# Six node tiles or four in the first phase of a two-layer graph network, the other two as a short group among the later ones

## The chip, the core and the metric

The kernel runs on one core of one Trainium2 chip. The metric is the device time of one execution in microseconds. Everything below comes from one program on one core, timed three times, and from one further execution that was recorded by the hardware profiler.

## What is computed

There are 4096 nodes with 512 features each and a sparse 4096 x 4096 adjacency matrix of float32 weights. Two layers follow each other, and each adds its result to x:

```python
h = jnp.maximum(_layernorm(x, axis=-1), 0.0)
x = x + _L0_gnn_ref(h, adj, L0_gnn_W, L0_gnn_b)
h = jnp.maximum(_layernorm(x, axis=-1), 0.0)
x = x + _L1_gnn_ref(h, adj, L1_gnn_W, L1_gnn_a, L1_gnn_wtrans)
```

The first layer is a dense product with the normalised adjacency:

```python
rowsum = adj.sum(axis=1)
d_inv_sqrt = jnp.where(rowsum > 0, rowsum ** (-0.5), 0.0)
normalized_adj = d_inv_sqrt[:, None] * adj * d_inv_sqrt[None, :]
return jax.nn.relu(normalized_adj @ x @ W + b)
```

The second layer is graph attention over the nonzero entries of the adjacency: `softmax(where(adj > 0, leaky_relu(Wh1 + Wh2.T), -1e12))` and its negative counterpart, each multiplied with the node features, joined and multiplied with `wtrans`, and an elu.

## The kernel before

**Tiles.** The 4096 nodes are 32 node tiles of 128 nodes. Layer 0 computes, for each destination tile i, the sum over the 32 source tiles j of adj_t[j, i] times y0[j], where y0[j] is d[j] times (normalised x[j]) W. W is multiplied first (`project`), d is applied when the product leaves the accumulator (`scale`, line 708).

**The list that the change edits.** `GROUPS` (line 24) says in which order and in what portions the destination tiles are worked: (first tile, number of tiles). Before, it is one group of six (tiles 26 to 31), six groups of four and one of two.

**First phase (lines 927 to 990), the first entry of GROUPS.** It runs once over the 32 source tiles j. For each j it reads the row tile of the adjacency (four loads of 512 KB, `ar`, on SP's queue) to sum the degrees, reads x[j] (GpSimd's queue), normalises and transposes it on TensorE (`turn_x`), multiplies with W (`project`, 4 matmuls of 128x512), and multiplies the first group's adjacency columns with y0[j] (`multiply`, line 858, one matmul of 128x512 for each node tile in the group). The columns come as one load `at` for each j, as wide as the group, from a pool of five buffers. Each accumulator of the first group holds one of the eight PSUM banks through the whole phase; `turn_x` and `project` use the banks that are left.

**Later groups (`group`, line 1038).** All y0 are there by now, and the product is done in 2x2 blocks by a seven-product scheme: two source tiles and two destination tiles at a time, seven products of 128x128x256 for what would be four of 128x128x512. The loop goes over 16 pairs of source tiles, jp. With four destination tiles, one jp is 14 products; with two it is 7. VectorE makes the sums of adjacency blocks that the scheme needs (`sum_at`, four operations for each load), and in the first such group the sums of y0 too (`sum_y`). A load `at` is 512 KB in either case: two source tiles by four destination tiles, or four by two (`nj = 8 // n`). The pool has six such buffers.

**What a group does for the one before it.** At the start of a group, VectorE joins the accumulators of the group before (`join_blocks`, or `evict` for the first phase) into one y per node tile. In the following steps jp = 0, 1, ... `finish0` turns each y into the node's new row: it adds x, writes `x1_dram`, takes the layer norm (line 642, ScalarE), makes two dot products (line 822, VectorE) and writes the row into eight copies of a table, one write on GpSimd's queue and seven on ScalarE's (`put_row`, line 443). The row is held in a tile `h` with two buffers, so the third row of a group can be made only when the first one's eight writes have landed. At jp = 8 `spread_s` (line 837) transposes the dot products of the finished tiles on TensorE; this matmul needs the dots of all of them.

**Masks.** `pack` turns each adjacency load into bytes (ScalarE, line 722; VectorE in the first phase, line 724) and writes them to the tables. `EARLY` (line 26) names three groups whose masks are made ahead of their turn, in the group with the given index, from loads of their own.

**Order.** A scheduler orders the instructions of each engine within what the program allows; [...] a DMA issue on ScalarE's or SP's list stands in that list like any other instruction.

**After layer 0.** Neighbour lists made in the groups with index 3 and 5 (`make_lists`) feed gathers from the tables, and `sparse_layer1` does the attention for 31 pairs of row blocks.

Of the kernel before, what the change touches and what calls it, by code (L numbers as in the profile page):

```python
# [8 lines left out]
F32 = mybir.dt.float32  # L9
# [10 lines left out]
P = 128  # L20
IB = 512


GROUPS = ((26, 6), (16, 4), (20, 4), (0, 4), (4, 4), (8, 4), (12, 4), (24, 2))

EARLY = {(24, 2): (2,), (12, 4): (3,), (8, 4): (4,)}
PAIR0 = 16
Y_PARTS = (8, 11, 13)
T_PARTS = (7, 9)
# [230 lines left out]
def gcn_gat_kernel(  # L260
# [24 lines left out]
    N, F = x.shape  # L285
# [15 lines left out]
    TT = RPT * RB // P  # L301
    late0, n_late = GROUPS[-1]
    tab0 = PAIR0 // TT
# [8 lines left out]
    def bank(name):  # L312
        return ps.tile([P, 512], F32, tag="ps", name=name)
# [4 lines left out]
    with sbuf(name="init", bufs=1) as init:  # L318
        column = init.tile([P, P], F32, name="column")
        nc.vector.memset(column[:, 0:1], 0.0)  # L320
        n = 1
# [120 lines left out]
    def put_row(queue, g, j, h):  # L442
        return queue.dma_start(  # L443
            out=rows_of(g, j // EJ)[:, j % EJ, :ROW_W], in_=h.bitcast(I32)
        )
# [77 lines left out]
    with sbuf(name="y0", bufs=1) as y_pool, sbuf(name="wa", bufs=1) as wa_pool, sbuf(name="bits", bufs=4) as bits_pool, sbuf(name="small0", bufs=4) as small, ExitStack() as rest, ExitStack() as lists:  # L523
# [16 lines left out]
        keys, lst = {}, {}  # L540
# [206 lines left out]
        def mark():  # L747
            while marking:
                tc.keep_in_program_order(marking.pop(0)())
# [5 lines left out]
        def affine(y, acc, j):  # L755

            nc.vector.scalar_tensor_tensor(y, acc, d_all[:, j : j + 1], b_bc, ALU.mult, ALU.add)
            return y

        def new_y(work, j, k):  # L760
            if k < 0:
                return work.tile([P, F], F32, tag="y", name=f"y{j}", bufs=4)
            if k == 0:
                spare.append(make_pool.tile([P, 3, F], F32, tag="keys", name="spare"))
            return spare[0][:, k]

        def evict(i0, acc, work, _):

            return {
                i0 + k: affine(new_y(work, i0 + k, k - 3), a, i0 + k) for k, a in enumerate(acc)  # L770
            }

        def join_blocks(i0, n, acc, work, new_w):

            ys = {}
            for x in range(n // 2):
                p16, p23, p45, p7 = acc[x]
                j0, j1 = i0 + x, i0 + n // 2 + x
                ys[j0], ys[j1] = y, v = [new_y(work, j, -1) for j in (j0, j1)]
                w = new_w(f"w{j0}")[:, :H]  # L780
                nc.vector.tensor_copy(y[:, :H], p16[:, :H])
                nc.vector.tensor_tensor(w, p16[:, H:], y[:, :H], ALU.add)  # L782
                nc.vector.tensor_tensor(y[:, H:], p45[:, H:], w, ALU.add)

                def first(p23=p23, y=y):
                    nc.vector.tensor_tensor(y, p23, y, ALU.add)

                def second(p7=p7, w=w, p45=p45, v=v):
                    two = "p (a f) -> p a f"
                    nc.vector.tensor_tensor(w, p7, w, ALU.add)  # L790
                    nc.vector.tensor_tensor(
                        v.rearrange(two, a=2),
                        p45.rearrange(two, a=2),
                        w.unsqueeze(1).to_broadcast([P, 2, H]),
                        ALU.add,
                    )

                if n == 2:
                    first()
                    affine(y, y, j0)  # L800
                    second()
                    affine(v, v, j1)
                else:
                    second()
                    first()
            if n > 2:
                for j, y in ys.items():
                    affine(y, y, j)
            return ys

        def finish0(work, j, y, h, prod):
# [15 lines left out]
            put_row(nc.gpsimd, tab0, j, h)  # L827
            if all(not j0 <= j < j0 + n for j0, n in GROUPS[-2:]):
                for g in others:
# [96 lines left out]

        i0, n = GROUPS[0]
        with sbuf(name="w0", bufs=1) as w0_pool, sbuf(name="ain", bufs=9) as ain, sbuf(name="xs", bufs=5) as x_pool, sbuf(name="at6", bufs=5) as at_pool, sbuf(name="bits6", bufs=3) as bits6, sbuf(name="ln", bufs=3) as ln_pool:
# [39 lines left out]
            acc = [bank(f"acc{i0 + k}") for k in range(n)]  # L968
            for j in range(NJ):
# [18 lines left out]
                pack(bits6, i0, j, ats.pop(j), j < 2)  # L988
                mark()
        pending = (GROUPS[0], partial(evict, i0, acc))  # L990
        listing, joining, spare = [], [], []

        def make_lists(g):
            make_keys(g)

            def rows_and_joins(c):
                count_listed(g, c, lst[g])
                li = table_rows(g, c, lst[g])
                joining.extend(partial(join, g, li, m) for m in range(c * NE, (c + 1) * NE))
                if c == 2:  # L1000
                    joining.append(partial(deal, g))

            for n, (c, r) in enumerate(steps):
                listing.append(partial(list_round, keys[g], lst[g], n))
                if n == 5:
                    listing.append(partial(make_places, g))
                if r + 1 == CAPS[c] // 8:
                    listing.append(partial(rows_and_joins, c))

        def judge():  # L1010
# [25 lines left out]
            return verdict  # L1036

        def group(b, work, at_pool, sum_pool, step, prod, n_h=2):

            nonlocal pending  # L1040
            i0, n = GROUPS[b]
            nj = 8 // n
            (p0, pn), take = pending
            order = [p0 + k for k in ((0, 2, 1, 3) if b > 1 else range(pn))]
            ats, sums = {}, {}

            def prepare(jp):
                if 2 * jp % nj == 0:
                    ats[jp] = load_at(at_pool, i0, n, 2 * jp, nj)
                    sums[jp] = sum_at(sum_pool, ats[jp], n, f"sums{i0}_{jp}")  # L1050
                else:
                    ats[jp], sums[jp] = ats[jp - 1], sums[jp - 1]
                if b == 1:
                    sum_y(jp)

            prepare(0)
            for j in order[:2]:
                if j not in xrs:
                    load_xr(j)
            for jp in range(NP):  # L1060
                if jp + 1 < NP:
                    prepare(jp + 1)
                mark()
                if jp == 0:
                    ys = take(work, prod)
                    p7 = bank(f"p7_{i0}")
                    acc = [
                        [*(bank(f"p{k}_{i0 + x}") for k in (16, 23, 45)), p7[:, x * H : (x + 1) * H]]
                        for x in range(n // 2)
                    ]  # L1070
                multiply_blocks(acc, n, jp, ats[jp], sums[jp])
                if (i0, n) not in EARLY:
                    pack(bits_pool, i0, 2 * jp, ats[jp])
                for (e0, m), when in EARLY.items():
                    if b in when:
                        pack(bits_pool, e0, 2 * jp, load_at(at_pool, e0, m, 2 * jp, 2))
                if jp < pn:
                    j = order[jp]
                    h = work.tile([P, ROW_W], F32, tag="h", name=f"h{j}", bufs=n_h)
                    finish0(work, j, ys.pop(j), h, prod)  # L1080
                    if jp + 2 < pn:
                        load_xr(order[jp + 2])
                if jp == 8:
                    spread_s(p0, pn)
                if jp == NP - 4:
                    for k in (0, n // 2):
                        load_xr(i0 + k)
                step(jp)
            pending = (GROUPS[b], partial(join_blocks, i0, n, acc))

# [5 lines left out]
        make_pool = lists.enter_context(sbuf(name="make", bufs=1))  # L1096
        with sbuf(name="work0", bufs=2) as work, sbuf(name="sums", bufs=3) as sum_pool, sbuf(name="at", bufs=6) as at_pool:

            def prod(name):
                return work.tile([P, F], F32, tag="q", name=name, bufs=1)  # L1100

            for b in range(1, len(GROUPS) - 1):

                def step(jp):
                    if jp == 2 and b in (3, 5):
                        make_lists((1, 0)[b == 5])
                    for _ in range((2, 3)[b == 6] if jp != 2 else 0):
                        if listing:
                            listing.pop(0)()
                    if joining:  # L1110
                        joining.pop(0)()

                group(b, work, at_pool, sum_pool, step, prod)
            while listing:
                listing.pop(0)()
            while joining:
                joining.pop(0)()
# [7 lines left out]
        with sbuf(name="work2", bufs=2) as work, sbuf(name="sums2", bufs=2) as sum_pool, sbuf(name="at2", bufs=4) as at_pool, sbuf(name="scratch", bufs=1) as scratch, sbuf(name="pair", bufs=1) as pair:  # L1125
# [100 lines left out]
            k = late0 % EJ  # L1226
# [204 lines left out]
```

## Time and profile before

| what | value |
|---|---|
| time before, median of 3 runs | 2124.37 us (2120.07 to 2126.74) |
| the profiled execution's own time | 2135.61 us |
| its span, first to last instruction | 2133.8 us |
| TensorE busy over the span | 2010.4 us (94%) |
| VectorE, ScalarE, GpSimd busy | 53%, 24%, 43% |
| first phase, to the last line-858 matmul | 336 us |
| groups of four and the group of two | 336 to about 1037 us |
| attention layer at its steady pace | 1330 to 2134 us |

The stage borders are read from where the matmuls of line 858 end and where those of line 899 begin and end. Time outside the span is 1.8 us. The page's busy time of TensorE counts modelled ends of pipelined matmuls; the distance from one matmul's start to the next is the safer measure of its cost. In this profile one float32 matmul shows as two records.

### The profile page before, as it was taken

Reading aid. Unit: us, or ns where it says so; the run is one execution under the profiler, and the core shown is the slowest. Engines: PE = TensorE matmul, PEld = TensorE weight load, DVE = VectorE, ACT = ScalarE, POOL = GpSimd, SP = SyncE. Lnnn points to the kernel's source line nnn. Section 1 sums busy time; section 2 is a strip of 40 time slices with the busy share of each in tenths; the row PEclk is TensorE's granted clock in tenths of the full one; section 3 lists DMA queues with packets and bytes.
Section 4 is the critical chain, followed back from the end, with each engine's and each line's share of the span. In section 5 each row is a group of like instructions: output and inputs, shape, how many; then the busy total and the mean of one; then the engine's idle time right before and its main releaser. Section 6 shows DMA issues by size and latency. Waiting matters only on the chain.

```text
span 2133.8 us, 20055 instructions
## 1 busy us (share of the span) xinstructions
PE 2010.4 (94%) x6456; PEld 1184.6 (56%) x6456; DVE 1121.2 (53%) x2805; ACT 511.8 (24%) x876; POOL 923.9 (43%) x988
## 2 busy tenths in 40 slices
PE   6999999999898989899878998999999999999998
PEld 3444447888787768787434443444444444444443
DVE  5444526463896469835644435445445445445441
ACT  4645612223232310001111212122122122122120
POOL 2010001111123310322467667777777777677740
PEclk9999999999999999999989999999999999999999
DMA  9988918786977875556587778888888888887850
GB/s 372 372 309 320 365 47 281 266 305 199 344 241 251 260 258 172 169 167 199 164 284 238 241 227 265 262 281 243 276 254 272 248 276 246 239 247 235 239 168 21
DMA packets 188041, 524.12 MB, mean 246 GB/s; under 512 B 25235, under 2 KB 34419, under 8 KB 187926
## 3 DMA queue, kind: packets, MB, share of 16 engines
q0 software_dynamic: 71296, 275.22, 41.7%
q1 hardware_dynamic: 88480, 196.46, 27.1%
q10 hardware_dynamic: 28150, 51.07, 6.7%
q8 instruction: 52, 0.85, 0.2%
q14 instruction: 63, 0.52, 0.1%
HBM read 430.83 MB, written 102.92 MB: 250 GB/s over the span
## 4 chain that ended last, share of the span: by engine, by line
PE 47%; DVE 6%; DMA 4%; POOL 4%; issue 3%; ACT 1%; ACTq 1%; another core or an unknown queue 0%; DVEq 0%; SPq 0%; POOLq 0%
PE u L1306 30%; PE o L1329 10%; PE p L899 5%; POOL g L457 4%; DMA at<-in_adj_t 2%; DMA g<-table,idx 1%; DVE keys L393 1%; PE tp L514 1%; DVE lst L391 1%; DMA table<-h 1%; ACTq L443 1%; PE u L1182 1%; ACT m L722 1%; DVE p L488 0%
## 5 line engine op out<-in xcount | busy, mean ns | idle before, releaser
L457 POOL DMA_INDIRECT g<-table,idx x704 | 753.4, 1070 | 266.6 <-issue 197.6
L1306 PE MATMUL u<-g,p 128*128 128x512 f32 x1736 | 766.7, 598 | 14.9 <-DVE p L488 9.7
L1306 PEld LDWEIGHTS u<-g,p 128*128 128x128 f32 x1736 | 326.8, 191 | 405.5 <-issue 382.2
L469 DVE TENSOR_TENSOR z<-g,s 128x512 f32<-128x512 f32 (+1 forms) x124 | 77.4, 624 | 422.6 <-DMA g<-table,idx 376.0
L899 PE MATMUL p<-t,sums 128*128 128x256 f32 x832 | 249.7, 385 | 15.9 <-DVE sums L887 12.8
L899 PE MATMUL p<-y,sums 128*128 128x256 f32 x832 | 253.6, 387 | 6.3 <-DVE sums L889 5.5
L899 PE MATMUL p<-y,at 128*128 128x256 f32 x832 | 253.9, 387 | 3.9 <-DMA at<-in_adj_t 2.6
L1329 PE MATMUL o<-wt_sb,ut 128*128 128x512 f32 x512 | 230.5, 603 | 0.9 <-ACT ut L518 0.5
L479 ACT ACTIVATE p<-z 128x896 f32<-128x896 f32 (+2 forms) x136 | 116.1, 903 | 313.3 <-DVE z L475 156.7
L899 PEld LDWEIGHTS p<-t,sums 128*128 128x128 f32 x832 | 160.1, 193 | 39.5 <-DVE sums L887 14.0
L899 PEld LDWEIGHTS p<-y,sums 128*128 128x128 f32 x832 | 161.5, 194 | 31.1 <-DVE sums L889 6.3
L899 PEld LDWEIGHTS p<-y,at 128*128 128x128 f32 x832 | 160.1, 194 | 30.9 <-issue 3.4
L858 PE MATMUL acc<-y,at 128*128 128x512 f32 x384 | 174.9, 593 | 2.4 <-ACT y L708 2.4
L488 DVE SCALAR_TENSOR_TENSOR p<-g,p 128x384 f32<-128x384 uint8 (+1 forms) x256 | 143.6, 620 | 60.8 <-ACT p L479 30.4
L733 POOL DMA_DIRECT2D table<-m x71 | 54.3, 766 | 251.9 <-ACT m L722 146.6
L1329 PEld LDWEIGHTS o<-wt_sb,ut 128*128 128x128 f32 x512 | 96.7, 194 | 111.9 <-issue 111.0
L722 ACT ACTIVATE m<-at 128x1024 uint8<-128x1024 f32 (+1 forms) x110 | 105.0, 987 | 181.2 <-DMA at<-in_adj_t 140.2
L899 PE MATMUL p<-t,at 128*128 128x256 f32 x416 | 127.0, 388 | 18.8 <-DVE w L782 17.7
L685 PE MATMUL yp<-w_sb,hx_t 128*128 128x512 f32 x256 | 122.2, 623 | 18.1 <-ACT y L708 15.8
L1315 ACT ACTIVATE us<-u,rl 128x512 f32<-128x512 f32 x62 | 42.5, 686 | 389.4 <-issue 237.8
L858 PEld LDWEIGHTS acc<-y,at 128*128 128x128 f32 x384 | 70.5, 190 | 80.5 <-issue 76.9
L886 DVE TENSOR_TENSOR sums<-at 128x256 f32<-128x256 f32 x104 | 43.3, 416 | 136.4 <-PE p L899 67.3
(183 smaller groups left out, 1720.3 us busy)
## 6 DMA issues: line engine op xcount, KB each, us to landing
at<-in_adj_t SPq DMA_DIRECT2D x136, 512.0 KB
ar<-in_adj SPq DMA_DIRECT2D x128, 512.0 KB
table<-h ACTq DMA_DIRECT2D x182, 258.0 KB
table<-m POOLq DMA_DIRECT2D x55, 256.0 KB
at<-in_adj_t SPq DMA_DIRECT2D x32, 384.0 KB
g<-table,idx POOLq DMA_INDIRECT x704
xr<-in_x SPq DMA_DIRECT2D x32, 256.0 KB
x<-x1d SPq DMA_DIRECT2D x32, 256.0 KB
```

The costliest lines, as they stand in the source:

```text
L457: nc.gpsimd.indirect_dma_start(out=gt[:, k, :], out_offset=None, in_=table[2 * n // RPT], in_offset=bass.IndirectOffsetOnAxis(ap=idx[n // ...
L469: return nc.vector.tensor_tensor(z, t.to_broadcast([P, n, RB]), s.unsqueeze(1).to_broadcast([P, n, RB]), ALU.add)
L479: i = nc.scalar.activation(p[:, :, g, :], z, AF.Exp, scale=(1.0, -1.0)[g])
L488: nc.vector.scalar_tensor_tensor(e, m, 0.0, e, ALU.is_gt, ALU.mult)
L685: nc.tensor.matmul(yp, hx_t[j][:, c * P : (c + 1) * P], w0_sb[:, c, :], start=c == 0, stop=c == FC - 1,)
L722: nc.scalar.activation(m, at, AF.Sign)
L733: nc.gpsimd.dma_start(out=rows_of(t, e)[:, c:, ROW_W + (a - t * TT) * P // 4 : ROW_W + (b - t * TT) * P // 4], in_=masks[i0][:, c:, (a - i ...
L858: nc.tensor.matmul(a, at[:, 0, it * P : (it + 1) * P], y0[j], start=j == 0, stop=j == NJ - 1)
L886: op(t[:, 0], a[:, :, 0, 1], a[:, :, 1, 1], ALU.add)
L899: i = nc.tensor.matmul(out, left[:, x * P : (x + 1) * P], right, start=jp == 0 and first, stop=jp == NP - 1 and (final or not first),)
L1306: nc.tensor.matmul(u, p[:, k0 + k].rearrange("p g c -> p (g c)"), gt[:, k, :F].bitcast(F32), start=k0 + k == 0, stop=k0 + k == nk - 1,)
L1329: nc.tensor.matmul(po, ut[:, g, c, :], wt_sb[:, g * FC + c, :], start=g == 0 and c == 0, stop=g == 1 and c == FC - 1,)
```

## The change

The first phase takes tiles 28 to 31 only. Tiles 26 and 27 become a group of two, third in the list, between (16, 4) and (20, 4). The groups after it keep their order, and the indices in `EARLY` and in the code that makes the lists move by one, so that this work stays with the same groups. `pack` is called once for each load, which matters only for a group of two that isn't in `EARLY`. The four y of the first phase fit in the four ordinary buffers, so the spare tile goes.

```diff
-GROUPS = ((26, 6), (16, 4), (20, 4), (0, 4), (4, 4), (8, 4), (12, 4), (24, 2))
-
-EARLY = {(24, 2): (2,), (12, 4): (3,), (8, 4): (4,)}
+GROUPS = ((28, 4), (16, 4), (26, 2), (20, 4), (0, 4), (4, 4), (8, 4), (12, 4), (24, 2))
+
+EARLY = {(24, 2): (3,), (12, 4): (4,), (8, 4): (5,)}
...
-        def new_y(work, j, k):
-            if k < 0:
-                return work.tile([P, F], F32, tag="y", name=f"y{j}", bufs=4)
-            if k == 0:
-                spare.append(make_pool.tile([P, 3, F], F32, tag="keys", name="spare"))
-            return spare[0][:, k]
+        def new_y(work, j):
+            return work.tile([P, F], F32, tag="y", name=f"y{j}", bufs=4)
...
-            order = [p0 + k for k in ((0, 2, 1, 3) if b > 1 else range(pn))]
+            order = [p0 + k for k in ((0, 2, 1, 3) if b > 1 and pn == 4 else range(pn))]
...
-                if (i0, n) not in EARLY:
+                if (i0, n) not in EARLY and 2 * jp % nj == 0:
                     pack(bits_pool, i0, 2 * jp, ats[jp])
...
-                    if jp == 2 and b in (3, 5):
-                        make_lists((1, 0)[b == 5])
-                    for _ in range((2, 3)[b == 6] if jp != 2 else 0):
+                    if jp == 2 and b in (4, 6):
+                        make_lists((1, 0)[b == 6])
+                    for _ in range((2, 3)[b == 7] if jp != 2 else 0):
```

More of the change, by code (lines that the diff above doesn't have):

```diff
@@ L758, in affine @@
             return y
-        def new_y(work, j, k):
-            if k < 0:
-                return work.tile([P, F], F32, tag="y", name=f"y{j}", bufs=4)
-            if k == 0:
-                spare.append(make_pool.tile([P, 3, F], F32, tag="keys", name="spare"))
-            return spare[0][:, k]
+        def new_y(work, j):
+            return work.tile([P, F], F32, tag="y", name=f"y{j}", bufs=4)
         def evict(i0, acc, work, _):
             return {
-                i0 + k: affine(new_y(work, i0 + k, k - 3), a, i0 + k) for k, a in enumerate(acc)
+                i0 + k: affine(new_y(work, i0 + k), a, i0 + k) for k, a in enumerate(acc)
             }
@@ L778, in join_blocks @@
                 j0, j1 = i0 + x, i0 + n // 2 + x
-                ys[j0], ys[j1] = y, v = [new_y(work, j, -1) for j in (j0, j1)]
+                ys[j0], ys[j1] = y, v = [new_y(work, j) for j in (j0, j1)]
                 w = new_w(f"w{j0}")[:, :H]
@@ L990, in gcn_gat_kernel @@
         pending = (GROUPS[0], partial(evict, i0, acc))
-        listing, joining, spare = [], [], []
+        listing, joining = [], []
         def make_lists(g):
```

## The prediction

> **What bounds the kernel now.** I began with the page's busy slices, to see which stages there are, and then cut the part that the change touches into stretches (columns: length, busy time and instructions of TensorE, its weight loads, VectorE, ScalarE, GpSimd, then TensorE's granted clock, DMA share, GB/s).
>
> ```profile
> 25.00:60.00 35.00, 31.64 (x84) 14.34 (x85) 20.27 (x73) 23.94 (x53) 5.28 (x9) 1.00 1.02 392
> 60.00:100.00 40.00, 38.65 (x102) 17.25 (x100) 18.90 (x57) 21.32 (x46) 3.83 (x6) 1.00 0.98 363
> 100.00:140.00 40.00, 35.18 (x88) 15.76 (x89) 16.68 (x52) 22.15 (x48) 3.84 (x6) 0.96 0.87 320
> 140.00:180.00 40.00, 34.47 (x88) 15.44 (x87) 17.91 (x53) 20.46 (x44) 3.70 (x6) 0.96 0.93 328
> 180.00:220.00 40.00, 36.96 (x96) 16.66 (x95) 17.47 (x51) 21.34 (x46) 3.70 (x6) 0.97 0.87 325
> 220.00:260.00 40.00, 38.90 (x102) 17.82 (x101) 18.34 (x58) 23.40 (x49) 3.17 (x5) 0.98 0.96 360
> 260.00:300.00 40.00, 40.00 (x110) 18.71 (x109) 11.91 (x25) 12.57 (x24) 3.02 (x4) 1.00 0.38 121
> 300.00:336.00 36.00, 36.00 (x87) 14.99 (x87) 16.62 (x45) 5.59 (x7) 0.90 (x3) 1.00 0.25 78
> 433.00:530.00 97.00, 97.00 (x451) 84.95 (x450) 50.16 (x141) 26.17 (x37) 15.35 (x26) 1.00 0.80 262
> ```
>
> The reader is to see that the first phase ends on TensorE: from 260 us the adjacency is in (DMA 0.38, then 0.25) and TensorE works alone, without a gap, to 336. Before that the DMA engines are nearly full too, and TensorE stands idle for 235 - 215.8 = 19.2 us of 25 to 260, 8.2%. In the group at 433 to 530 TensorE has no gap at all. Second view: who waits for whom, in the first phase (SP's queue from 0 to 340, the others from 100 to 260).
>
> ```profile
> SPq L846 <- PE acc L858: 120.2, 19, 9.8
> ...
> DVE sta L433 <- DMA xt<-in_x: 71.6, 15, 7.0
> ...
> PE yp L685 <- ACT y L708: 14.6, 6, 4.8
> ```
>
> SP holds the stream back for 120 us, waiting for TensorE to release column buffers: TensorE sets the pace. Its own gaps come from the other side: VectorE stands in its list at the statistics of an x that hasn't landed, the degree chain behind it is late, and so is y0 (line 708).
>
> Third view: ScalarE in order of time in the group at 434, which finishes four rows.
>
> ```profile
> 442.14 0.81 ACT L642 ACTIVATE h<-y,rrb 128x512 f32<-128x512 f32 x1 [0.46 <-DVE rrb L639]
> 443.83 6.56 ACTq L443 DMA_DIRECT2D table<-h  x7
> ...
> 453.17 6.21 ACTq L443 DMA_DIRECT2D table<-h  x7
> 459.48 0.81 ACT L642 ACTIVATE h<-y,rrb 128x512 f32<-128x512 f32 x1 [5.53 <-DMA table<-h]
> ...
> 461.16 9.58 ACTq L443 DMA_DIRECT2D table<-h  x7
> 470.84 0.81 ACT L642 ACTIVATE h<-y,rrb 128x512 f32<-128x512 f32 x1 [9.08 <-DMA table<-h]
> ...
> 472.52 5.26 ACTq L443 DMA_DIRECT2D table<-h  x7
> ```
>
> Four rows take a fixed time, set by 28 table writes issued by ScalarE and by the two h buffers, however long the group is.
>
> **What the Trainium skill says.** "TensorE: Matmul & The Clock Gate", section "What's actually happening": the clock is halved by default and is released after about 3.4 us of sustained work. The trace agrees: a gap from 974.9 to 978.6 is followed by a granted clock of 0.80, 0.50 and 0.85 in the next three slices of 2 us. "DMA: Bandwidth & Descriptors", section "Issuing engines are not separate DMA queues": SP's, ScalarE's and GpSimd's transfers share the same 16 DMA engines. The trace agrees in kind: with the adjacency stream at a share of 0.9 and more, x on GpSimd's queue is late up to 7.0 us. "PSUM — Partial Sum Buffer", "Specifications (TRN2)": 8 banks; before, six accumulators leave two for everything else of the first phase, after, four.
>
> **The change part by part.** All against the profiled execution: span 2133.8, own time 2135.6, which is 11.2 above the median of the runs shown; I carry the difference over to the median.
>
> 1. *Removed from the first phase: 2 x 32 = 64 matmuls of 128x512.* Weight loads of line 858 start at 327.17, 327.60, ... 335.76: 0.43 us apart, two records a matmul, 0.86 us each; 64 x 0.86 = 55.0 us of TensorE. All of it is on the path in 260 to 336. With it go 4.2 MB of columns, and 32 mask conversions on VectorE shrink from 768 to 512 columns (0.55 us now); these lie beside TensorE and count as nothing while it sets the pace.
>
> 2. *What is late next in the first phase.* TensorE is busy 292.0 us from 25 to 336.2; without the 64 it is 237.0. The stream: 90.4 MB came in by 260 (the rates above, summed); less the columns left out by then, about 87.5 MB, at 392 GB/s (25 to 60) some 226 us, with a tail of sums, y0 and the last products behind it. So TensorE (262 without any gap) and the stream (226 to 250 with what it loses at lower rates) become nearly equal, and gaps stay likely. Two more free banks would let `project` run ahead over late y0: at most the 14.6 us. Against it, with TensorE at 7.4 us per source tile and the stream at about 7, there is hardly any lead left to cover a late x. I take the share of gaps as it is, 8.2%, over the whole: 237.0 / 0.918 = 258.1, end at 283.1, a gain of 53.1 us. Bounds: 2.5% of gaps, end at 268, gain 68; 12%, end at 294.3, gain 42.
>
> 3. *Added: the group (26, 2).* 16 x 7 = 112 products of 128x256. From 336.61 to 390.57 there are 125 of them without a gap: 0.4317 us each; 48.4 us, and 0.3 for its own `spread_s`: 48.7. On the path in full, as TensorE is. Beside it: 8 loads of 512 KB on SP, 32 block sums (0.42 us each, 13.4) and a join on VectorE, 8 conversions (1.06 us) on ScalarE, 8 mask writes on GpSimd that were there before in the first phase. VectorE has some 40 us of work in it; the sums for the first four jp stand before the join in the compiled order, which covers it.
>
> 4. *The wait that this adds.* The four rows of (16, 4) were finished in a 97 us group and are now finished in the 48 us one. `spread_s` comes after 75 of the 112 products in the compiled order, 75 x 0.4317 = 32.4 us after the group's start. When is the fourth row's second dot done? In the group above (first product at 434.5 by counting) it ended at 473.4: +38.9. The compiled order of the short group is worse: rows two and three are normalised together, then 14 writes follow, then row four. First row at +9.8, dot 10.8, seven issues 6.6, landing about 6 (the chain of waits has 4.2, 5.8 and 8.2 for such a write), row three 24.2, a conversion 1, 14 issues of 0.98 (mean of the four groups of seven above) 13.8, row four 39.8, dots 41.5: a wait of 9.1. The other reading gives 6.5. I take 7.8, bounds 4 and 13. Behind it on TensorE stand 37 products; VectorE stands before the same row with the last sums; ScalarE has the masks of the next group behind it, whose loads are six buffers ahead.
>
> 5. *After the wait the clock is low.* At 978 to 984 20 records ran where 33 would: about 2.4 us lost for a gap of 3.7, part of it the gap's end. I take 2.5, bounds 1 and 4.
>
> 6. *Edits at nothing.* Group (20, 4) finishes two rows instead of four, but had no gap that could go. The indices only keep work with its group. The first phase's y in ordinary buffers: all four are free then. Handover from the first phase and two borders in place of one: VectorE did eight of the 16 `sum_y` in the 260 to 336 tail, which gets short; 1.0 us, bounds 0 and 4.
>
> Sum: -53.1 + 48.7 + 7.8 + 2.5 + 1.0 = +6.9. Span 2140.7; at the median, 2131.3 us.
>
> **Rivals.**
> - *The gain and the loss cancel.* Two more banks take away half of the gaps: end at 276, gain 60; 60 against 60.0: 2124. For it: line 685 waits on banks. Against: the stream has no slack.
> - *Faster, one mechanism: TensorE and stream overlap almost perfectly in the first phase.* End at 268, gain 68, and the fourth row 5 us late, clock 1.5: -68 + 48.7 + 5 + 1.5 + 1 = -11.8, 2112.6. It decides from an end of the first phase before about 270. For it: 55 us less on the engine that holds SP back for 120. Against: gaps of 8% though the stream was held back.
> - *Much slower.* Gaps of 12% (gain 42), row four at +46 (wait 13.6, clock 3): +24, 2148. For it: a full DMA makes x late and table writes land late, 8.2 us here.
> - *The change doesn't do what it says.* The compiled order has 128 direct products in the first phase and the 112 new ones; I give it nothing.
>
> **How the numbers follow.** Chances: forecast 0.34, much slower 0.16, cancel 0.28, faster 0.22. A measurement of this kernel can tell about 0.3%, 6.4 us, from no change; the forecast lies just beyond it. Slower 0.50, same 0.28, faster 0.22. Range: from the faster case to the much slower one, 2112 to 2148, which leaves about one in ten outside at each end; the forecast's own range is 2127 to 2139.
>
> **What would show it.** Right: line-858 matmuls end near 283; line 837 in the short group stands about 8 us behind line 822, with the clock at half after it; the groups from (20, 4) on look as before, shifted. Wrong: an end of the first phase before 270 or after 295; no gap at that line 837; new gaps in later groups, which I count as unchanged.

## The result

| what | before | after |
|---|---|---|
| median | 2123.8 us (2120.1 to 2126.7, 4 runs) | 2108.4 us (2106.8 to 2111.6, 4 runs) |
| ratio of the times | 1 | 0.9926, 95% interval 0.9905 to 0.9946 |
| span of the profile | 2133.8 us | 2107.2 us |
| last accumulating matmul of the first phase ends | 336.8 us | 276.4 us |

The change makes the kernel 15.4 us faster; the forecast was 6.9 us slower. Two later measurements, on two chips, gave ratios of 0.9926 and 0.9933 (below). The profile of before was taken some 11 us above its median, so the two spans are not compared directly. All lines of the code past the cut stand four lines higher after the change: 858 is now 854, 837 is 833, 899 is 895, 822 is 818, 782 is 778.

The first phase after the change, in stretches (length, then busy time and instructions of TensorE, its weight loads, VectorE, ScalarE, GpSimd, TensorE's granted clock, DMA share, GB/s):

```profile
25.00:60.00 35.00, 30.04 (x77) 13.94 (x78) 18.32 (x69) 21.05 (x47) 4.44 (x8) 0.95 1.02 396
60.00:100.00 40.00, 38.19 (x104) 17.51 (x103) 21.38 (x68) 25.25 (x53) 3.45 (x6) 1.00 0.93 333
100.00:140.00 40.00, 40.00 (x113) 18.91 (x112) 22.10 (x73) 27.48 (x60) 4.74 (x8) 1.00 1.01 387
140.00:180.00 40.00, 40.00 (x110) 18.70 (x109) 20.33 (x63) 25.21 (x53) 3.44 (x6) 1.00 1.02 385
180.00:220.00 40.00, 32.91 (x79) 13.73 (x78) 16.26 (x50) 19.25 (x43) 2.38 (x4) 0.93 0.71 245
220.00:260.00 40.00, 40.00 (x107) 18.55 (x106) 19.14 (x52) 28.19 (x55) 1.67 (x4) 0.98 0.92 348
260.00:276.40 16.40, 16.40 (x38) 5.85 (x36) 10.14 (x31) 1.26 (x2) 0.00 (x0) 1.00 0.22 60
sum 251.40, PE 237.53 PEld 107.19 DVE 127.66 ACT 147.68 POOL 20.11; mean PE 33.93 PEld 15.31 DVE 18.24 ACT 21.10 POOL 2.87
```

TensorE's busy time is 237.5 us, and 237.0 was forecast: the products removed cost what was said. Its idle time is 251.4 - 237.5 = 13.9 us, where the forecast put 21.1 and the kernel before had 19.2. From 100 to 180 us TensorE has no gap although the DMA engines are full. Who waits for whom, 0 to 270 us (total, times, longest), on TensorE and then in SP's queue:

```profile
PE tx L654 <- ACT hx L642: 10.8, 3, 6.0
PE yp L685 <- DVE hx_t L660: 8.2, 4, 2.5
PE acc L854 <- ACT y L708: 5.5, 5, 2.4
```

```profile
SPq L666 <- ACT ar L675: 52.3, 35, 6.4
```

The waits of the projection (line 685) for y, 14.6 us before from 100 to 260 us, are gone, and so are SP's 120 us behind column buffers that TensorE still reads. Three other waits have grown: for the normalised x that is to be transposed (line 654; 8.1 us before), of the projection for the transposed x (2.3 us before) and of the products for y (2.4 us before). The longest of them, 6.0 us, stood in the kernel before too.

The short group, ScalarE in order of time (start, length; DMA issues of its queue are marked ACTq). Its first product starts at 374.8:

```profile
383.04 0.81 ACT L642 ACTIVATE h<-y,rrb 128x512 f32<-128x512 f32 x1 [0.45 <-DVE rrb L639]
384.73 6.41 ACTq L443 DMA_DIRECT2D table<-h  x7
...
392.43 0.80 ACT L642 ACTIVATE h<-y,rrb 128x512 f32<-128x512 f32 x1
396.57 0.81 ACT L642 ACTIVATE h<-y,rrb 128x512 f32<-128x512 f32 x1 [3.35 <-DMA at<-in_adj_t]
...
397.52 12.37 ACTq L443 DMA_DIRECT2D table<-h  x12
409.94 0.81 ACT L642 ACTIVATE h<-y,rrb 128x512 f32<-128x512 f32 x1 [11.61 <-DMA table<-h]
```

And TensorE where it meets the attention vectors of these four rows:

```profile
412.54 0.56 PE L833 MATMUL s_ps<-ident,s_all 128*4 128x128 f32 x2 [5.16 <-DVE t_all L828]
413.03 1.22 PE L895 MATMUL p<-y,sums 128*128 128x256 f32 x2
414.04 1.06 PE L895 MATMUL p<-t,sums 128*128 128x256 f32 x2
414.90 1.06 PE L895 MATMUL p<-y,at 128*128 128x256 f32 x2
415.75 0.74 PE L895 MATMUL p<-t,sums 128*128 128x256 f32 x2
416.32 0.59 PE L895 MATMUL p<-t,at 128*128 128x256 f32 x2
```

The fourth row follows 14 issues, as foreseen, and TensorE arrives as foreseen (32.6 us after the group's start; 32.4 said). But the fourth row's h starts at +35.1 us, not +39.8, so the wait is 5.2 us and not 7.8. Behind it four products take 3.3 us instead of 1.7: a loss of 1.6 us, not 2.5.

To place the rest I use the matmul `s_ps`, one for each finished group, as a mark. Times are counted from the end of the first phase; "before" has the two profiles of that kernel, "after" the three of the changed one.

| mark | before | after | moved by |
|---|---|---|---|
| end of first phase, from the start | 336.8, 337.5 | 276.4, 272.0, 272.5 | -63.5 |
| in group (20,4) | 152.3, 153.4 | 208.7, 208.4, 207.6 | +55.4 |
| in group (0,4) | 259.7, 260.7 | 309.0, 313.2, 308.0 | +49.9 |
| in group (8,4) | 485.8, 488.1 | 539.1, 543.0, 538.0 | +53.1 |
| the last one | 713.0, 719.8 | 762.5, 770.0, 767.6 | +50.3 |

So there are three departures from the forecast: 10.4 us in the first phase, 4.6 us in the short group (60.0 forecast with the handover), and 5.5 us between the marks in (20,4) and (0,4), which was to be unchanged. The third is less certain as part of the total: about 3 us of it are lost again by the mark in (8,4) (TensorE's waits for the join behind (0,4) grew from 4.5 to 5.9 us on average), and they return by the last mark, where profiles of one kernel lie up to 7 us apart.

### The profile page after: what moved, and what is told of

The parts are those of the page before. It is cut to its first block, busy times and chain, and to the rows that moved or that the text cites. A ratio compares the mean times of both kernels' runs of the same rounds, so it can differ in the third digit from the quotient of the medians.

```text
span 2107.2 us, 20420 instructions
## 1 busy us (share of the span) xinstructions
PE 1996.8 (95%) x6554; PEld 1202.9 (57%) x6554; DVE 1131.9 (54%) x2851; ACT 519.2 (25%) x885; POOL 919.5 (44%) x988
## 4 chain that ended last, share of the span: by engine, by line
PE 46%; DVE 6%; POOL 5%; DMA 5%; issue 3%; ACT 1%; ACTq 0%; DVEq 0%; POOLq 0%
PE u L1302 29%; PE o L1325 9%; PE p L895 5%; POOL g L457 5%; DMA g<-table,idx 2%; DVE keys L393 1%; PE tp L514 1%; DVE lst L391 1%; DMA ld<-li,off 1%; PE u L1178 1%; DMA at<-in_adj_t 1%; DMA table<-h 1%; DVE p L488 0%; ACTq L443 0%; DMA table<-m 0%
## 5 line engine op out<-in xcount | busy, mean ns | idle before, releaser
L1302 PE MATMUL u<-g,p 128*128 128x512 f32 x1736 | 763.1, 597 | 11.2 <-DVE p L488 11.2
L895 PE MATMUL p<-t,sums 128*128 128x256 f32 x896 | 268.8, 385 | 13.2 <-DVE sums L883 13.2
L895 PE MATMUL p<-y,at 128*128 128x256 f32 x896 | 272.8, 387 | 3.9 <-DMA at<-in_adj_t 3.7
L895 PE MATMUL p<-y,sums 128*128 128x256 f32 x896 | 272.1, 386 | 1.6 <-DVE sums L885 1.6
L895 PEld LDWEIGHTS p<-t,sums 128*128 128x128 f32 x896 | 173.1, 194 | 39.3 <-DVE sums L883 15.4
L895 PEld LDWEIGHTS p<-y,at 128*128 128x128 f32 x896 | 172.1, 194 | 31.6 <-ACT m L722 3.6
L895 PEld LDWEIGHTS p<-y,sums 128*128 128x128 f32 x896 | 173.4, 194 | 26.5 <-DVE sums L885 2.0
L722 ACT ACTIVATE m<-at 128x1024 uint8<-128x1024 f32 (+1 forms) x118 | 113.6, 992 | 219.4 <-DMA at<-in_adj_t 160.6
L895 PE MATMUL p<-t,at 128*128 128x256 f32 x448 | 135.9, 386 | 20.1 <-DVE w L778 20.1
L854 PE MATMUL acc<-y,at 128*128 128x512 f32 x256 | 121.4, 599 | 5.6 <-ACT y L708 5.5
L413 POOL DMA_INDIRECT ld<-li,off x48 | 43.2, 900 | 158.1 <-DMA ld<-li,off 103.7
```

Of the source, the lines that this page charges most:

```text
L722: nc.scalar.activation(m, at, AF.Sign)
L854: nc.tensor.matmul(a, at[:, 0, it * P : (it + 1) * P], y0[j], start=j == 0, stop=j == NJ - 1)
L895: i = nc.tensor.matmul(out, left[:, x * P : (x + 1) * P], right, start=jp == 0 and first, stop=jp == NP - 1 and (final or not first),)
L1302: nc.tensor.matmul(u, p[:, k0 + k].rearrange("p g c -> p (g c)"), gt[:, k, :F].bitcast(F32), start=k0 + k == 0, stop=k0 + k == nk - 1,)
```

## The experiments

They were made on several chips, on which the kernel before takes 2122.7 to 2144.6 us; each is therefore read by its ratio to the kernel before on the same chip, and against the changed kernel's ratio. 0.001 is 2.1 us.

### The kernels themselves again

> The changed kernel once more, as the yardstick of the three runs beside it. If the gain of the result holds on this chip, the ratio to the kernel before is 0.9905 to 0.9946 (about 15 us less). Its trace is a second look at the marks that the theories argue from: end of the first phase 276 us (+-2), the matmul s_ps of the short group's third boundary at 412.5 behind a wait of 5 us, and 72.5 us from there to the matmul s_ps of group (20,4). If the 7.6 us that the groups behind the short one gained were an accident of one profile, these marks lie within 3 us of those of the kernel before: 107 to 109 us between the marks of (20,4) and (0,4) and not 100.

Measured: 0.9926 (0.9903 to 0.9948), end of the first phase 272.0, the wait at `s_ps` 4.9 us, and 104.8 us between the marks of (20,4) and (0,4), where the first profile has 100.3 and the third 100.4.

> The changed kernel a third time, as the yardstick of this call: ratio to the kernel before 0.9926 +- 0.002, end of the first phase 270 to 277 us, the sums that TensorE waits for at the border behind (20,4) 286 to 288 us behind that end.

Measured: 0.9933 (0.9910 to 0.9956), 272.5, sums 285.1 us behind the end, 1 us earlier than expected.

> The kernel before once more, for a second profile. The profile shown of it was taken in an execution 11 us above its median; in it 1,082 us passed from the first matmul of the attention stage to the end, against 1,066 in the profile of the changed kernel and 1,083 in the second profile of the changed kernel. If the attention stage is the same in both kernels and its length only differs between executions and chips, this profile shows an attention stage within 4 us of that of the other kernels of this call, and the whole gain lies ahead of it: 10 to 13 us at the start of that stage. If the change does shorten the attention stage, this one is 5 us or more above the others'.

Measured: 0.9996 (0.998 to 1.0013); last mark at 1057.3 of a span of 2143.3. From that mark to the end it is 1,086 us, and 1,085 in the second and 1,084 in the third profile of the changed kernel. The attention stage is the same in both; the 16 us that the first two profiles differ by there belong to the executions. At the last mark the second profiles differ by 15.3 us, near the difference of the medians; the first two differ by 10.9 there, and the means over all profiles of the two kernels by 13.2.

### Two banks held: the first phase

```diff
+            hold = [bank(f"hold{k}") for k in range(2)]
             for j in range(NJ):
...
+                for spare in hold if j in (0, NJ - 1) else ():
+                    nc.tensor.matmul(
+                        spare[:, 0:1], ats[j][:, 0, :P], y0[j][:, 0:1], start=j == 0, stop=j == NJ - 1
+                    )
...
+            held = small.tile([P, 2], F32, tag="held", name="held", bufs=1)
+            for k in range(2):
+                nc.vector.tensor_copy(held[:, k : k + 1], hold.pop(0)[:, 0:1])
```

> The changed kernel, but two further PSUM banks are kept occupied through the whole first phase (four matmuls of one column each write them, at its first and its last step), so that transposes and projections again share two banks as in the kernel before; the output does not change. Theory of the banks: the two banks that became free took away the waits of the projections for y, so the first phase ends 6 to 7 us later than in the changed kernel (282 to 284), waits 'yp <- ACT y' of 10 us or more are back, and the time is 5 to 7 us above the changed kernel's. Rival, that the stream of columns is no longer held back by TensorE, or that the smaller tiles leave TensorE fewer delays: end of first phase within 1.5 us of 276, time within 2 us. Rival, that a shorter step exposes the next limit whatever the banks: in between, 2 to 4 us.

Measured: 0.9957 (0.9943 to 0.9971), 6.6 us above the changed kernel beside it; the intervals overlap by 0.0005. The first phase ends at 281.8. In the thirteen profiles here of kernels with the banks free and five column buffers it ends between 270.4 and 276.4. TensorE's waits in this kernel, 0 to 282 us, and the sum of its stretches from 25 to 281.8:

```profile
PE yp L685 <- ACT y L708: 14.3, 9, 3.5
PE tx L654 <- ACT hx L642: 6.6, 2, 6.2
...
PE yp L685 <- DVE hx_t L660: 2.5, 1, 2.5
PE acc L854 <- ACT y L708: 2.4, 1, 2.4
```

```profile
sum 256.80, PE 238.03 PEld 107.02 DVE 128.84 ACT 149.09 POOL 20.12; mean PE 34.00 PEld 15.29 DVE 18.41 ACT 21.30 POOL 2.87
```

This is the list of waits of the kernel before, 0 to 335 us:

```profile
PE yp L685 <- ACT y L708: 15.8, 7, 4.8
PE tx L654 <- ACT hx L642: 8.1, 3, 6.0
...
PE acc L858 <- ACT y L708: 2.4, 1, 2.4
PE yp L685 <- DVE hx_t L660: 2.3, 1, 2.3
```

The projection waits for y, because the bank that it needs is the one that y is still read out of. The idle time is 256.8 - 238.0 = 18.8 us, against 19.2 before. With the banks free, the projection runs ahead; 14 us of waits go, some 10 come back as waits for the transposed x and for y in the products themselves, and 4 to 5 us remain as gain. The stream is as free here as in the changed kernel: SP waits 1.0 us in all for the accumulating matmuls of TensorE, not 120. The clock was low early in this profile (0.85 from 25 to 60 us), behind a first wait of 2.4 us and one of 3.5 us for y; four of the thirteen other profiles also ran at half rate behind that first wait and yet ended at 272.7 to 274.1. The second and third profiles of the changed kernel gain as much again in busy time (232.8 and 232.3 us up to the end at 272, with the clock at 1.00 in every stretch, where before it was at 0.96 to 0.98 from 100 to 260). That this part belongs to the banks isn't shown: from 60 us on the clock was at 1.00 with the banks held, too.

### Three column buffers: the stream

```diff
-        ... sbuf(name="at6", bufs=5) as at_pool ...
+        ... sbuf(name="at6", bufs=3) as at_pool ...
```

> The changed kernel with three column buffers in the first phase and not five. The held banks brought back 6.5 us, which leaves the stream's part open. Rival theory of the first phase: in the kernel before, the queue of the stream stood 120 us behind column buffers that TensorE still read, and 0 in the changed kernel; if this mattered, holding it back again ends the first phase 4 us or more later (280 or above, against 272 to 276) and costs as much in time. Theory of the banks: TensorE is the bound there, the stream runs ahead far enough with three buffers too: end of first phase within 3 us of 276, time within 3 us of the changed kernel's.

Measured: 0.9958 (0.9934 to 0.9982); the first phase ends at 277.4, and SP stands 73 us behind TensorE again. That end is 1 us above the highest and 4 above the mean (273.3) of the thirteen. The time is higher than expected, but 3 us of it is a wait of 12.2 us at the border behind (0,4), where the changed kernel has 8.7 to 9.5. So the stream accounts for 1 to 4 us of the first phase at most; it is the smaller part, and this run alone doesn't separate it from the spread. With the stream free and the banks held, above, the first phase ended 8 us behind that mean.

### The spread moved late: the short group

```diff
-                if jp == 8:
+                if jp == (NP - 1 if n == 2 and b < len(GROUPS) - 1 else 8):
```

> The changed kernel, but in the short group the spread of the attention vectors (the matmul s_ps and what follows it) is issued at the last of its 16 steps and not at step 8, when the fourth row's dots are long done. If the wait of 5.2 us and the low clock behind it were a real price of the short group: no wait at s_ps there, group (20,4) begins 6 to 7 us earlier, time 5 to 7 us below the changed kernel's. Rival, that the wait only moves (VectorE is behind with the sums or with the joining of the next border, so TensorE waits there for it instead): the wait at s_ps is gone but group (0,4) begins within 2 us of before, time within 2 us.

Measured: 0.9926 (0.9901 to 0.9951), nothing gained. The wait at `s_ps` is gone, and the mark in (20,4) comes 202.6 us behind the first phase, 5.6 us earlier than the mean of 208.2: that is about what wait and clock really cost. Some 84 us further it is given back. A product early in (0,4) shows it, first with the late spread, then in the kernel before, then in the changed kernel (TensorE in order of time: start, length, and the wait before it):

```profile
561.97 1.22 PE L895 MATMUL p<-y,sums 128*128 128x256 f32 x2 [6.27 <-DVE sums L885]
```

```profile
570.66 1.22 PE L899 MATMUL p<-y,sums 128*128 128x256 f32 x2 [5.48 <-DVE sums L889]
```

```profile
562.45 0.70 PE L895 MATMUL p<-y,sums 128*128 128x256 f32 x2 [1.64 <-DVE sums L885]
```

Counted from the end of the first phase, VectorE's sums release this product at 286.5 with the late spread, at 286.1, 287.5 and 285.1 in the changed kernel, and at 233.9 and 235.3 before. At this place VectorE sets the time. It moved by 51.6 us where TensorE moved by 55.4, so TensorE's own wait shrank: 5.5 and 6.2 us before, 1.6, 3.3 and 1.7 after. That is 3.6 us on average; with a clock that stays up after the shorter wait in two of three profiles, it is most of the 5.5 us between the two marks.

### The short group one place later

```diff
-GROUPS = ((28, 4), (16, 4), (26, 2), (20, 4), (0, 4), (4, 4), (8, 4), (12, 4), (24, 2))
+GROUPS = ((28, 4), (16, 4), (20, 4), (26, 2), (0, 4), (4, 4), (8, 4), (12, 4), (24, 2))
...
-EARLY = {(24, 2): (3,), (12, 4): (4,), (8, 4): (5,)}
+EARLY = {(24, 2): (2,), (12, 4): (4,), (8, 4): (5,)}
```

> The changed kernel, but the short group stands behind (20,4) and not ahead of it (the masks of the last group are made in the group of the same place, one earlier in the count). Theory of the borders: the 7 us that group (20,4) gained came because it finishes two rows and not four while the lists of the second table are made; here that place is taken by (0,4), which then gains the 7 us, while the short group finishes four rows and keeps a wait at s_ps of 4 to 8 us: time within 2 us of the changed kernel's. Rival, that the gain belongs to the place in the order (the short group's low load before the lists are made lets VectorE catch up): it is lost, time 5 to 8 us above the changed kernel's.

Measured: 0.9920 (0.9897 to 0.9943), as the changed kernel. The wait at `s_ps` is 5.3 us, in its new place. (0,4) now finishes two rows while the first lists are made, and TensorE has no wait there at all; in (4,4) it waits 9.8 us for the sums, as before. So the gain doesn't hang on the short group standing ahead of (20,4). The expectation was wrong about where the lists are made in the changed kernel: in (0,4), not in (20,4).

### Three buffers for h

```diff
-        def group(b, work, at_pool, sum_pool, step, prod, n_h=2):
+        def group(b, work, at_pool, sum_pool, step, prod, n_h=3):
...
-                return work.tile([P, F], F32, tag="q", name=name, bufs=1)
+                return work.tile([P, F], BF16, tag="q", name=name, bufs=1)
```

> The changed kernel with three buffers for the finished row h in the groups and not two (room is made by keeping the unused product of the dots in half the width; the sums of the dots stay as they are). In the changed kernel ScalarE waits 18 us in group (20,4) and at the border behind it for table writes that still read an h, VectorE waits behind ScalarE's square root, and TensorE behind VectorE's sums. Theory that this chain sets the borders: the waits of ScalarE for the table go below 8 us there, the wait at s_ps in the short group shrinks or goes, time 4 to 10 us below the changed kernel's. Rival, that the borders are VectorE's own work or the stream of columns: waits 'sums' and 'w' at the borders as before, time within 2 us.

> Three buffers for h once more, beside the changed kernel in the same call. In the first run the wait at s_ps of the short group was gone, the mark of group (0,4)'s successor came 9 us earlier after the end of the first phase (420 and not 428 to 430), and the ratio was 0.9891 against 0.9926, with intervals that touch. If the gain is real: again 5 to 9 us below the changed kernel of this call. If it was an accident: within 3 us of it.

Measured: 0.9891 (0.9864 to 0.9918) and 0.9894 (0.9870 to 0.9918), 7.5 and 8.4 us below the changed kernel. The product of the dots, kept in half width to make room, saves nothing itself: the instructions of line 818 take 0.38 us on average in both kernels. No wait at `s_ps` is left in the short group: its fourth row no longer waits for a buffer. But the sums behind (20,4) still come 282.6 and 285.8 us after the first phase, and TensorE waits 5.1 and 6.3 us for them. The theory holds for the short group and not for that border.

The same with the late spread:

> Three buffers for h, and in the short group the spread of the attention vectors at its last step. Moving the spread alone gave nothing: TensorE came 6 us earlier to the border behind (20,4) and waited 7.8 us there for VectorE's sums, which came at the same 286 us behind the end of the first phase as in the changed kernel. If these sums hang on ScalarE's waits for h, both waits go: the sums come at 280 or earlier, time 6 to 12 us below the changed kernel's and more than with three buffers alone. If they hang on something else, the time is that of three buffers alone within 2 us.

Measured: 0.9919 (0.9891 to 0.9946), sums at 286.0 us. No gain on top of three buffers; the intervals are too wide to call it a loss.

### Table writes on other queues

Three of the seven writes of a row on GpSimd's queue, with two buffers for h, then with three:

```diff
-                for g in others:
-                    put_row(nc.scalar, g, j, h)
+                for k, g in enumerate(others):
+                    put_row((nc.scalar, nc.gpsimd)[k % 2], g, j, h)
```

> The changed kernel, but of the seven table writes that ScalarE's queue issues for each finished row, three go to GpSimd's queue. Theory: with the DMA engines full, seven issues hold ScalarE 7 to 9 us, its next square root waits behind them, VectorE's sums behind the square root, TensorE behind the sums; with four issues ScalarE is held 4 to 5 us, the wait at s_ps in the short group shrinks below 2 us, the sums at the border behind (20,4) come 3 us or more earlier than 286 us behind the first phase, and the time falls 3 to 8 us below the changed kernel's. Rival, that the DMA engines themselves are the limit (0.85 to 0.95 busy at the borders), so that it doesn't matter which queue waits: the waits of TensorE at the borders within 2 us of the changed kernel's, and so the time.

> Three buffers for h and three of the seven table writes on GpSimd's queue. If both waits of ScalarE count and are different ones, the gains add: 8 us or more below the changed kernel, and below three buffers alone by 3 us or more. If they are one and the same limit, the time is within 2 us of three buffers alone.

Measured: 0.9988 (0.9970 to 1.0007) and 0.9924 (0.9901 to 0.9948). Both lose, 11.8 and 6.4 us against the same kernel with one queue (the second with intervals that overlap): neither theory. ScalarE and GpSimd of the first of the two, at the border behind (0,4), show one place where the writes stand late:

```profile
690.36 0.81 ACT L642 ACTIVATE h<-y,rrb 128x512 f32<-128x512 f32 x1 [21.15 <-DMA table<-h]
```

```profile
684.37 0.86 POOL L413 DMA_INDIRECT ld<-li,off  x1 [0.79 <-DMA ld<-li,off]
685.24 2.23 POOL L443 DMA_DIRECT2D table<-h  x4
```

The writes stand in GpSimd's queue behind the list's indirect transfers, and an h buffer is free only when its last write has landed. TensorE waits 14.4 us there, against 8.7 to 9.5 in the changed kernel. But this explains little of the loss: ScalarE's wait for h is as long there in the changed kernel (21.5 to 22.0 us), and 11.2 us are lost already at the mark in (0,4), 321.3 against 310.1 on average. Behind (20,4), where the sums come at 294.7 us, no indirect transfer stands in GpSimd's list. What causes that part stays open.

The same split with SyncE in GpSimd's place:

> The changed kernel with three of the seven table writes of a row on SyncE's queue. SyncE has no list loads in it, so this is the cleaner form of the attempt with GpSimd's. Theory that ScalarE's held queue paces the sums behind (20,4): ScalarE's wait 'rrb <- table<-h' of 9 to 10 us there falls to about 5, the sums come 283 us or less behind the end of the first phase (286 to 287 in the changed kernel). Rival, that the DMA engines' total is the limit, or that columns now stand behind the table writes: the sums at 286 or later, time not below the changed kernel's.

Measured: 1.0045 (1.0027 to 1.0064), 25 us above the changed kernel. ScalarE's wait fell only to 8.2 us, and the sums came at 292.7 us. On SyncE the writes wait for an h inside the queue that carries the columns: 29.5 us in all from 380 to 720 us, 19.0 at longest. That this makes the loss is likely, but not shown.

### The first table's write moved to ScalarE

Even in the changed kernel one write of each row, into the first table, is on GpSimd's queue. The waits at the border behind (0,4) in its second profile, 660 to 690 us:

```profile
ACT h L642 <- DMA table<-h: 25.6, 2, 22.0
DVE prod L818 <- ACT rrb L638: 16.2, 1, 16.2
...
PE p L895 <- DVE sums L883: 9.5, 1, 9.5
```

```diff
-            put_row(nc.gpsimd, tab0, j, h)
+            put_row(nc.scalar, tab0, j, h)
```

> The changed kernel, but each finished row's write into the first table goes to ScalarE's queue and not to GpSimd's, where at the border behind (0,4) it stands behind the indirect loads of the lists: ScalarE waits 21.5 us there for a free h, VectorE 15.7 us for ScalarE, TensorE 8.7 us for the sums, in the kernel before (21.4, 15.6, 8.5) as in the changed one. Theory that this write holds the border: that wait of TensorE falls below 3 us, time 5 to 10 us below the changed kernel's. Rival, that with eight issues instead of seven ScalarE's queue is held longer and the wait stays or grows: time within 2 us, or above.

Measured: 0.9920 (0.9899 to 0.9940). The wait of 9.5 us became 5.3 us, but the ratio is only 0.0006 (1.3 us) below the changed kernel's, less than the interval can tell from nothing: a miss.

> Both: three buffers for h, and the write into the first table on ScalarE's queue. Three buffers alone were 7 to 8 us below the changed kernel. If the two remove different waits: 10 to 16 us below the changed kernel (ratio 0.985 to 0.988), the best of all. If three buffers had already hidden the write behind the lists: within 3 us of three buffers alone (0.989).

Measured: 0.9862 (0.9838 to 0.9885), 2091.9 us where the kernel before takes 2122.7 on the same chip: 13.6 us below the changed kernel's ratio, the lowest time of all, though its interval overlaps that of three buffers alone. TensorE's waits in it from 640 to 735 us:

```profile
PE p L895 <- DMA at<-in_adj_t: 2.4, 2, 1.9
PE p L895 <- DVE sums L883: 0.9, 2, 0.5
```

At this border one buffer more and the other queue are each half a remedy: TensorE waits 5.4 and 5.8 us for the sums with the buffer alone, 5.3 with the queue alone, at most 0.5 with both. A likely reason is that with two buffers ScalarE still waits for the eight writes that it issues itself (21.3 us), and with three for the one behind the lists (18.3 us).

## Why the prediction was wrong

**Step 1, right.** The 64 products were worth 55 us: busy time 237.5 us in the first profile, where 237.0 was forecast.

**Step 2 failed, and with it the sign.** "I take the share of gaps as it is, 8.2%": the gaps fell to 13.9 us (5.5%). The 8.2% were those of 25 to 260 us; over 25 to 336 the share had been 6.2%, so the step put more idle time than before (21.1 us against 19.2), not the same. The step had the mechanism in hand, two more free banks that let the projection run ahead of a late y, and set it aside because the stream would leave no lead. Holding the two banks shows that this was the wrong choice: with them held the first phase ends at 281.8, next to the forecast 283.1, with about the idle time and the same waits as before; with them free at 270.4 to 276.4. The stream ran at 385 GB/s and more beside a TensorE without gaps from 100 to 180 us. (Its own estimate of 226 us should have been 223, 87.5 MB at 392 GB/s; nothing hangs on it.) The term was -53.1 and measured -60.4 in the first profiles, -63.5 on average. Some 7 us of the 10.4 are idle time that didn't come, most of the rest the higher clock of two profiles. The rival "cancel" had named this end, 276, and its mechanism; with the forecast's other terms it would still have said no change.

**Step 3, right.** With 5.6 us off for wait and clock, the short group's 55.4 us leave 49.8, against 48.7 for its products and 1.0 for the handover.

**Steps 4 and 5, right in kind, too dear.** The place, its cause and TensorE's arrival were right. The wait was 5.2, 4.9 and 4.2 us and not 7.8, the lost clock 1.6 and not 2.5; moving the spread late shows 5.6 us for both where 10.3 stood. Row four came at +35.1 us and not +39.8: its 14 issues took 13.2 us, near the 13.8 said, but row one was 1.6 us earlier and rows two and three were ready sooner. The clock's term rested on a miscount: in 978 to 984 us 28 records fit at full rate (0.216 us each), not 33, so the 20 that ran mean 1.7 us and not 2.4. (The gap ahead of them ended at 978.8 us, not 978.6.)

**Step 6 failed in one point.** "Group (20, 4) finishes two rows instead of four, but had no gap that could go", and later groups "look as before, shifted". They don't: early in the next group, (0,4), TensorE already waited 5.5 us for VectorE's sums, and that wait took up part of the added work. What was inserted on TensorE moved VectorE's sums by 4 us less than TensorE, so 5.5 us between two marks went, 2 to 5 of which are left further on. That VectorE sets the time there is shown by the late spread, whose 5.6 us ended in exactly this wait. What paces the sums themselves stays open. In the trace ScalarE's square root waits 9 to 10 us there behind its own seven table issues (in the second profile they stand from 535.56 to 544.95, and it starts at 544.99), but three buffers for h, the late spread and every split of the issues left the sums between 280.6 and 294.7 us, and none of these runs moved them by removing that wait alone.

**The sum.** -63.5 + 55.4 - 5.1 up to the last mark is -13.2 us, against -15.4 in the medians; the forecast had -53.1 + 60.0 + 0. Of the 20 us between the two sums half is step 2, a quarter each steps 4 and 5 together and step 6. The 2108.4 us lie below the range of 2112 to 2148. The rival "faster" (2112.6) came nearest: it had the short group right, 5 us of wait and 1.5 of clock, put the first phase at 68 us where 63.5 came, and had nothing of step 6 either.

## What to carry to other kernels

When a change frees buffers, look up which waits were for those buffers and forecast with these waits gone, then ask what is late next; carrying over the idle share forecasts the old buffers. Work added to the bounding engine costs less than its length if that engine already waits for another one further on, and a wait removed ahead of such a place gains nothing: find the next place where another engine releases it, on both sides. A second queue for transfers is not free room: here splitting the writes lost time every time, so look first at what they would stand behind, and what would stand behind them.

## What was unexpected in the hardware

A wait of TensorE doesn't lower the clock by its length alone. Early in the first phase of all seventeen profiles stands the same wait of 2.44 us: twelve ran on at full rate behind it, five at half rate (1.01 and 0.85 us between records instead of 0.53 and 0.43). Another, of 3.86 us, stands in all of them between 948 and 988 us: half rate came with the first record in five, and 0.3 to 1.1 us later in twelve. In the kernel with writes on SyncE a wait of 4.4 us was followed by full rate for a product, and half rate came only behind the next wait, of 0.8 us, 2.3 us later. The Trainium skill, "TensorE: Matmul & The Clock Gate", section "What's actually happening", says that the activity window runs freely, so that the same work meets it differently; these waits agree.

Spreading one engine's transfer issues over two queues cost 12 us with GpSimd's and 25 us with SyncE's as the second. "DMA: Bandwidth & Descriptors", section "Issuing engines are not separate DMA queues", says of several issuing engines that they only save issue time; here, where the queues also carry waiting work, the split lost more than it saved.

The same kernel took 2122.7 us on one chip and 2144.6 on another, 1% more; only ratios on one chip could show effects of this size.
